# Weights' cycle of an eight-step software pipeline reordered, right products on two row tiles, and inverse roots by Newton steps

## The chip, the cores and the metric

The kernel runs on one core of a Trainium2 chip. The metric is the device time of one execution in microseconds (us), as the median over runs. TensorE is called PE, VectorE DVE, ScalarE ACT, GpSimd POOL and SyncE SP. SP computes nothing here: its queue issues nearly all DMAs.

## What is computed

A network of four layers on x of shape (4, 32, 32, 16), each `x = x + layer(groupnorm(x))`. Layers 0, 1 and 3 are position-dependent convolutions, layer 2 is an interval layer.

```python
# convolution layer (0, 1, 3): every position (i,j) has its own 3x3 kernel G[i,j] and its own weights W[i,j]
first   = einsum('ijyx,byxc->bijc', M, inputs)
shifted = conv(inputs, all 32*32*16 kernels of G)            # b, ij, yx, f
second  = einsum('ijyx,bijyxc->bijc', W, relu(inputs - shifted))
out     = first - second
# interval layer (2)
r = concat(running max, running min over intervals)          # b, 33, 33, 32
f = max_k sigmoid(f[b,i,k] @ Wf + r[b,k,j] @ Wr + b)         # two such steps
out = sigmoid(concat(f, r) @ W2 + b2)
# group norm
(g - mean) / sqrt(var + 1e-5)                                # 8 groups of two channels
```

## The kernel before

**Phases and steps.** Two groups of two batches and three convolution layers give six *phases* (`phases`, L90). A phase goes over eight blocks of 128 positions (`t`), a block over 16 channels `f` and 2 batches `b`: 32 *steps* a block, 256 a phase, 1536 in all. A step computes one tile `pc` of 128 positions x 1024 pixels: `first_part` multiplies it up in matmuls with WL and WU (L658 to L663) and has ACT scale it; `second_part`, run one step later, adds the matmuls with WD and W9 and has DVE form min(., 0) times the position's weights, with a sum over pixels (L680). Every matmul uses 64 rows; the two halves of the rows work as two row tiles side by side. Four `pc` tiles exist (two PSUM banks each), and the interval layer's small products take their tiles from the same ring.

**Units.** The kernels of four channels make a *unit*, used for eight steps. The kernel computes in a split fp32: each unit has a high and a low part of its weights. Units 0 and 1 are used plainly; from unit 2 on `prep_parts` (L220) builds a unit in a *cycle* of eight calls, one at the start of each step (L718). Unit u's cycle begins 15 steps ahead of its first use, and its call c (1 to 8) stands c steps after step 8(u - 2), so 16 - c steps ahead of that use. In the first block the cycle starts at step 3, and two steps take an extra call. The calls:

| call | before |
|---|---|
| 1 | DVE: mask the weights to their high bits (`high`, L203) |
| 2 | ACT: half of W9 (`halve`, L175) |
| 3 | ACT: WD (L236); POOL: WL (L237), W9 (L238) |
| 4 | ACT: WU (L240); POOL: WD (L241), four copies between quarters of the rows (L243, L245) |
| 5 | POOL: `prep` of the next unit (L214) |
| 7 | SP: two DMAs copy `parts[:, 0]` with its row halves swapped into `parts[:, 1]` (L251), the *swap*; then the raw load of unit u + 2 (L110) |

PE reads `parts[:, 1]` from the second pair of matmuls of the unit's first step. There are three buffers of `parts` and of W9, two of `raw`.

**Work behind.** All other work (norms, taps, interval layer, first terms) is a generator, `behind` (L733). At the end of a step it may be continued: `yield n` waits n steps, `yield IDLE` waits for a step whose call allows it (calls 1, 5, 6, 7, 8), `yield CALM` for one of the calls 6 to 8. So order on every engine and queue is program order, fixed by these yields; nothing is reordered. `before_conv` (L368) prepares the next phase: group norm, transposes to `xt` (L375), 8 DMAs to DRAM (`inner`, L381), 24 DMAs that read the nine shifted images back (`taps`, L392), and per batch a split and 12 DMAs that place the parts (`place`, L290). In the first phase `rest_of_start` (L869) does a split and a `place` for each batch of the first group.

**Norms.** `group_norm` (L312) takes sums on DVE, differences on POOL, then Sqrt on ACT (L358) and a reciprocal on DVE. A dummy Sqrt on `spare` (L353) and a dummy Sigmoid (L591) bring ACT's function table in ahead of use.

**Interval layer.** `right_side` (L555) multiplies the right factors in three matmuls of 11 values of k each (352, 231 and 110 columns), all on rows 0 to 63, each in its own PSUM tile and in its own step, and ACT copies each into `rt`.

Of the kernel before, what the change touches and what calls it, by code (L numbers as in the profile page):

```python
# [15 lines left out]
P = 128  # L16
# [28 lines left out]
def net_kernel(ctx: ExitStack, tc: tile.TileContext, x, xq, xi, convs, iv_w, iv_b, out):  # L45
# [162 lines left out]
    def prep(u, at=0, to=FU, eng=nc.gpsimd):  # L208
# [4 lines left out]
        for s in range(2 if u < PLAIN else 1):  # L213
# [4 lines left out]
            )  # L218

    def prep_parts():  # L220

        for u in range(PLAIN, n_chunks * NU):
            parts = wpool.tile([P, 2, 3, FU, P], F32R, tag="parts", bufs=AHEAD + 1, name=f"parts_{u}")
            W9 = wpool.tile([P, FU, P], F32R, tag="W9", bufs=AHEAD + 1, name=f"W9_{u}")
            units[u] = [parts[:, :, k] for k in range(3)] + [W9]
            src = raws.pop(u)
            w8 = src[:, 0].rearrange("p f k -> p (f k)")  # L230
            WU, WL, WD = (parts[:, 0, k].rearrange("p f k -> p (f k)") for k in range(3))
            high = upper(src[:, 0:1], 1, f"w{u}")[:, 0]
            yield (IDLE,)
            halve(W9, src[:, 1], low_w)
            yield ()
            nc.scalar.activation(WD, high, AF.Copy, scale=-EPS)  # L236
            nc.gpsimd.tensor_tensor(WL, w8, high, ALU.subtract)  # L237
            nc.gpsimd.tensor_tensor(W9, W9.bitcast(F32), src[:, 2], ALU.add)  # L238
            yield ()
            nc.scalar.copy(WU, high)  # L240
            nc.gpsimd.tensor_tensor(WD, WD.bitcast(F32), WL.bitcast(F32), ALU.add)  # L241
            for lo, hi in QUARTERS:
                nc.gpsimd.tensor_copy(WU[hi], WL[lo].bitcast(F32))  # L243
            for lo, hi in QUARTERS:
                nc.gpsimd.tensor_copy(WL[lo], high[hi])  # L245
            yield ()
            prep(u + 1)
            yield (IDLE,)
            yield (IDLE, CALM)
            for h in range(2):  # L250
                nc.sync.dma_start(  # L251
                    parts[64 * h : 64 * h + 64, 1].bitcast(F32),
                    parts[64 - 64 * h : 128 - 64 * h, 0].bitcast(F32),
                )
            load_raw(u + RAWS)
            yield (IDLE, CALM)
            yield (IDLE, CALM)

# [50 lines left out]
    def pair_view(ap):  # L309
        return ap.rearrange("p t (g s) -> p t g s", s=2)  # L310

    def group_norm(g, name, dst, gap):  # L312

# [104 lines left out]
    def first_terms(layer, mt):  # L418
# [27 lines left out]
    def constants():  # L446
# [6 lines left out]

        nc.gpsimd.tensor_scalar_mul(mask2[GC : 2 * GC], mask2[GC : 2 * GC], -1.0)
        yield 2
# [22 lines left out]
        for k, name in ((1, "r0"), (4, "r1")):  # L478
            t = const.tile([64, NQ * GB, C], F32, name=name)
            for q in range(NQ):  # L480
                blocks(t[:, q * GB : (q + 1) * GB, :], k, mask2, GB)
            iv[name] = t.rearrange("p k c -> p (k c)")
            yield 1
    def interval_layer(g):
# [37 lines left out]
        def running(dst, src):  # L522
# [17 lines left out]
            fill=0.0, base=0, channel_multiplier=0,  # L540
        )
        yield 5

# [11 lines left out]
        def right_side(name, wr):  # L555

            for k0 in range(0, T1, 11):
                j0 = k0 + 1
                ps = bank(f"ps_{name}{g}{k0}")
                n = T1 - j0  # L560
                nc.tensor.matmul(  # L561
                    ps[:, : 11 * n], lhsT=wr, rhs=r[:R, k0 : k0 + 11, j0:], start=True, stop=True
                )
                nc.scalar.copy(
                    rt[:, j0:, k0 : k0 + 11],
                    ps[:, : 11 * n].rearrange("p (k j) -> p j k", j=n),
                )
                yield 1

        def step(name, ftp, bias):  # L570
# [19 lines left out]
            yield IDLE  # L590
            nc.scalar.activation(spare, spare, AF.Sigmoid)  # L591
            yield 2
# [114 lines left out]
    def conv_layer(phase, behind):  # L707
# [4 lines left out]
        for t in range(NT):  # L712
# [267 lines left out]
```

## Time and profile before

| | |
|---|---|
| median of 3 runs | 2478.37 us (2478.1 to 2479.17) |
| the profiled execution | 2478.41 us |
| its span, first to last instruction | 2476.7 us |
| PE busy | 2458.2 us, 99% |
| DVE busy | 2087.3 us, 84% |
| ACT busy | 1878.4 us, 76% |
| POOL busy | 1579.7 us, 64% |
| ACT table loads | 5, 1283 ns each |
| swap DMAs (L251) | 380, 384 KB each, median 4.9 us from issue to landing |
| raw loads (L110) | 190, 768 KB each, 7.1 us |

Matmul ends are modelled, so PE's busy share is read together with the starts of the matmuls: a step begins every 1.566 us on PE in the steady part. In phase 3, step 224 begins on PE at 1600.3 us; times of other steps of that phase follow from it, since PE hardly waits there. A group's line gives line, engine, operation, output<-inputs, shapes, count, then busy time and mean, then the idle time before it and what ended it. A timeline line gives start and duration in us, engine, line, operation, output<-input and count; for "SPq" it is the time that SP took to issue the DMAs, waits between them included. A wait's line gives who waited for whom, then the total in us, how often, and the longest.

### The profile page before, as it was taken

The numbers are of one execution on the slowest core, as the hardware profiler recorded it, in microseconds if no ns is written. First come the engines' busy times: TensorE is split into PE (matmuls) and PEld (weight loads), VectorE is DVE, ScalarE is ACT, GpSimd is POOL, SyncE is SP. The second block draws the span as 40 slices with busy tenths as digits, with TensorE's granted clock in tenths as the row PEclk, the third lists the DMA queues.
The fourth block names the chain that finished last, engine by engine and source line by source line (L and its number), as shares of the span: only waits on it lengthen the run. The fifth ranks groups of instructions, "written<-read, shape, count | busy, mean of one in ns | idle before, by whom it ended". The sixth has DMA issues, their size and how long they took to land.

```text
span 2476.7 us, 58058 instructions
## 1 busy us (share of the span) xinstructions
PE 2458.2 (99%) x21906; PEld 2090.1 (84%) x21906; DVE 2087.3 (84%) x3617; ACT 1878.4 (76%) x2181; POOL 1579.7 (64%) x1750
## 2 busy tenths in 40 slices
PE   8999999999999999999999999999999999999999
PEld 5999888888888888888888988888998888888887
DVE  9888878888888888778898988899889888788887
ACT  4778767787777778777777777787777787677776
POOL 4766655666565657555567777586878676555552
PEclk9999999999999999999999999999999999999999
DMA  6446754466454467644454545574455467554442
GB/s 198 138 137 182 203 155 135 124 182 164 133 143 135 135 168 198 186 116 134 136 145 127 142 124 140 146 196 125 126 138 144 127 181 195 154 148 137 137 137 54
DMA packets 97673, 366.92 MB, mean 148 GB/s; under 512 B 26480, under 2 KB 31472, under 8 KB 97392
## 3 DMA queue, kind: packets, MB, share of 16 engines
q1 hardware_dynamic: 96832, 362.79, 53.0%
q8 instruction: 172, 2.82, 0.5%
q14 instruction: 109, 0.89, 0.1%
q10 hardware_dynamic: 432, 0.39, 0.1%
q0 software_dynamic: 128, 0.02, 0.0%
HBM read 199.78 MB, written 1.02 MB: 81 GB/s over the span
## 4 chain that ended last, share of the span: by engine, by line
PE 94%; DVE 2%; issue 1%; DMA 1%; ACT 0%; SPq 0%; POOL 0%; ACTq 0%; DVEq 0%; POOLq 0%
PE pc L627 93%; DVE junk L680 1%; PE pf L425 1%; DMA raw<-in_g 1%; ACT pc L663 0%; DMA first<-in_g 0%; SPq L298 0%; DVE raw L846 0%; SPq L300 0%; PE ps_l L548 0%; PE ps_r L561 0%; DMA parts<-parts 0%; DVE tables L508 0%; DVE raw L854 0%; DMA ib<-first 0%
## 5 line engine op out<-in xcount | busy, mean ns | idle before, releaser
L680 DVE SCALAR_TENSOR_TENSOR junk<-pc,WT 128x1024 f32<-128x1024 f32 x1536 | 1879.5, 1224 | 359.1 <-PE pc L627 308.3
L663 ACT ACTIVATE pc<-pc 128x1024 f32<-128x1024 f32 x1520 | 1532.0, 1008 | 561.0 <-PE pc L627 535.8
L627 PE MATMUL pc<-ib,parts 64*128 64x512 f32 x6080 | 958.5, 388 | 4.1 <-DVE junk L680 3.4
L627 PE MATMUL pc<-iyz,parts 64*128 64x512 f32 x6080 | 955.5, 387 | 2.2 <-ACT pc L663 2.0
L627 PE MATMUL pc<-ia,parts 64*128 64x496 f32 x6080 | 933.5, 379 | 0.0
L627 PEld LDWEIGHTS pc<-ia,parts 64*128 64x128 f32 x6080 | 595.5, 184 | 100.8
L627 PEld LDWEIGHTS pc<-ib,parts 64*128 64x128 f32 x6080 | 591.5, 184 | 105.0 <-DVE junk L680 9.9
L627 PEld LDWEIGHTS pc<-iyz,parts 64*128 64x128 f32 x6080 | 592.5, 184 | 88.4 <-ACT pc L663 6.4
L627 PE MATMUL pc<-im,W 64*128 64x496 f32 x3072 | 611.5, 384 | 0.0
L237 POOL TENSOR_TENSOR parts<-raw,upper_w 128x512 fp32r<-128x512 f32 x190 | 248.5, 1308 | 500.2 <-DVE upper_w L203 434.8
L627 PEld LDWEIGHTS pc<-im,W 64*128 64x128 f32 x3072 | 303.0, 184 | 54.5 <-issue 3.2
L243 POOL CAST parts<-parts 32x512 fp32r<-32x512 f32 x380 | 231.1, 608 | 50.1 <-ACT parts L240 31.8
L238 POOL TENSOR_TENSOR W<-W,raw 128x512 fp32r<-128x512 f32 x190 | 247.6, 1303 | 1.8 <-ACT W L175 1.8
L241 POOL TENSOR_TENSOR parts<-parts 128x512 fp32r<-128x512 f32 x190 | 246.8, 1299 | 2.0 <-ACT parts L236 1.9
L245 POOL CAST parts<-upper_w 32x512 fp32r<-32x512 f32 x380 | 231.6, 609 | 22.8
L214 POOL TENSOR_TENSOR raw<-raw,ident 128x512 f32<-128x512 f32 x190 | 199.9, 1052 | 52.2 <-DMA raw<-in_g 28.7
L175 ACT ACTIVATE W<-raw,low_w 128x512 fp32r<-128x512 f32 x190 | 136.2, 717 | 0.1
L680 DVE DVE_READ_ACCUMULATOR junk<-pc,WT 128x1 f32 x1536 | 127.5, 83 | 0.0
L236 ACT ACTIVATE parts<-upper_w 128x512 fp32r<-128x512 f32 x190 | 118.8, 625 | 6.6 <-DVE upper_w L203 6.4
L240 ACT CAST parts<-upper_w 128x512 fp32r<-128x512 f32 x190 | 116.5, 613 | 0.0
L695 POOL TENSOR_SCALAR acc<-acc 128x32 f32<-128x32 f32 x40 | 16.4, 409 | 141.7 <-DVE junk L680 139.7
L203 DVE TENSOR_SCALAR upper_w<-raw 128x512 int32<-128x512 int32 x190 | 86.1, 453 | 1.2 <-POOL raw L214 0.9
(139 smaller groups left out, 479.4 us busy)
## 6 DMA issues: line engine op xcount, KB each, us to landing
raw<-in_g SPq DMA_DIRECT2D x190, 768.0 KB, 7.1
parts<-parts SPq DMA_DIRECT2D x380, 384.0 KB, 4.9
WT<-in_w SPq DMA_DIRECT2D x48, 512.0 KB, 4.6
MT<-in_mt SPq DMA_DIRECT2D x24, 512.0 KB, 7.4
raw<-xs SPq DMA_DIRECT2D x120, 71.8 KB, 2.9
ib<-temp SPq DMA_DIRECT2D x40, 128.0 KB, 2.6
ia<-temp SPq DMA_DIRECT2D x80, 62.0 KB, 3.4
ib<-first SPq DMA_DIRECT2D x8, 128.0 KB, 2.4
```

Of the source, the lines that this page charges most:

```text
L175: nc.scalar.activation(dst, src, AF.Copy, scale=mask[:, 1:2])
L214: eng.tensor_tensor(raws[u][:, s, at:to], raws[u][:, s, at:to], pick[s][:, f0 + at : f0 + to].unsqueeze(2).to_broadcast([P, to - at, P]), ...
L236: nc.scalar.activation(WD, high, AF.Copy, scale=-EPS)
L237: nc.gpsimd.tensor_tensor(WL, w8, high, ALU.subtract)
L238: nc.gpsimd.tensor_tensor(W9, W9.bitcast(F32), src[:, 2], ALU.add)
L240: nc.scalar.copy(WU, high)
L241: nc.gpsimd.tensor_tensor(WD, WD.bitcast(F32), WL.bitcast(F32), ALU.add)
L243: nc.gpsimd.tensor_copy(WU[hi], WL[lo].bitcast(F32))
L245: nc.gpsimd.tensor_copy(WL[lo], high[hi])
L627: nc.tensor.matmul(ps[:, h, at : at + n], lhsT=w[r], rhs=v[r] if n == NH else v[r][:, :n], start=first and k == 0, stop=k == len(pairs) - ...
L663: nc.scalar.activation(ps, ps, AF.Copy, scale=1.0 + EPS)
L680: nc.vector.scalar_tensor_tensor(junk, ps.rearrange("p h n -> p (h n)"), 0.0, chunks[n], op0=ALU.min, op1=ALU.mult, accum_out=accs[phase][ ...
```

## The change

The weights' cycle has the same number of calls and of operations, in a new order:

| call | after |
|---|---|
| 1 | ACT: half of W9 |
| 2 | DVE: `high`, in a tile of its own; SP: the swap of the *previous* unit |
| 3 | ACT: WD; POOL: WL |
| 4 | ACT: WU; POOL: W9, `prep` of the next unit |
| 5 | POOL: WD, the four copies; SP: the raw load of unit u + 2 |

`IDLE` is now allowed at calls 2, 5, 6, 7, 8. The norm's inverse root is a shift and a subtraction on the bits (DVE), followed by four Newton steps of four small operations each on POOL; the dummy Sqrt, the Sqrt and the reciprocal go, and with them two of the yields. A single dummy Sigmoid in layer 0's `first_terms` takes the place of those in the interval steps. The right factors' weights are laid on all 128 rows, the table `r` is copied to rows 64 to 127 (`below`), and the three right matmuls are issued together, the first on the upper rows, the other two on the lower, into one pair of banks. `squares` lies in the buffer of `junk`.

```diff
+    def exchange(parts):
+        if parts is not None:
+            for h in range(2):
+                nc.sync.dma_start(
+                    parts[64 * h : 64 * h + 64, 1].bitcast(F32),
+                    parts[64 - 64 * h : 128 - 64 * h, 0].bitcast(F32),
+                )
...
+        swapped = None
         for u in range(PLAIN, n_chunks * NU):
...
-            high = upper(src[:, 0:1], 1, f"w{u}")[:, 0]
-            yield (IDLE,)
             halve(W9, src[:, 1], low_w)
             yield ()
+            high = work.tile([P, FU * P], F32, tag="high", bufs=2, name=f"high_{u}")
+            nc.vector.tensor_scalar(
+                high.bitcast(I32), w8.bitcast(I32), HIGH, None, op0=ALU.bitwise_and
+            )
+            exchange(swapped)
+            yield (IDLE,)
             nc.scalar.activation(WD, high, AF.Copy, scale=-EPS)
             nc.gpsimd.tensor_tensor(WL, w8, high, ALU.subtract)
-            nc.gpsimd.tensor_tensor(W9, W9.bitcast(F32), src[:, 2], ALU.add)
             yield ()
             nc.scalar.copy(WU, high)
+            nc.gpsimd.tensor_tensor(W9, W9.bitcast(F32), src[:, 2], ALU.add)
+            prep(u + 1)
+            yield ()
             nc.gpsimd.tensor_tensor(WD, WD.bitcast(F32), WL.bitcast(F32), ALU.add)
...
-            yield ()
-            prep(u + 1)
+            load_raw(u + RAWS)
+            swapped = parts
             yield (IDLE,)
-            yield (IDLE, CALM)
-            for h in range(2):
-                nc.sync.dma_start(
...
-            load_raw(u + RAWS)
-            yield (IDLE, CALM)
-            yield (IDLE, CALM)
+            for _ in range(3):
+                yield (IDLE, CALM)
+        yield (IDLE, CALM)
+        exchange(swapped)
...
+    def inverse_root(v, name):
...
+        nc.gpsimd.tensor_scalar(a, v, 1.0 / (2 * NP), 1e-5, op0=ALU.mult, op1=ALU.add)
+        nc.vector.tensor_scalar(
+            t.bitcast(I32), a.bitcast(I32), 1, None, op0=ALU.logical_shift_right
+        )
+        nc.vector.tensor_scalar(
+            y.bitcast(I32), t.bitcast(I32), -1.0, float(0x5F3759DF), op0=ALU.mult, op1=ALU.add
+        )
+        nc.gpsimd.tensor_scalar_mul(a, a, -0.5)
+        for pause in (1, 1, IDLE, 2):
+            yield pause
+            nc.gpsimd.tensor_tensor(t, a, y, ALU.mult)
+            nc.gpsimd.tensor_tensor(t, t, y, ALU.mult)
+            nc.gpsimd.tensor_scalar(t, t, 1.5, None, op0=ALU.add)
+            nc.gpsimd.tensor_tensor(y, y, t, ALU.mult)
+        return y
...
-        nc.scalar.activation(spare, spare, AF.Sqrt)
         v = yield from totals(f"v{name}")
-        yield 2
-        yield IDLE
-        rstd = work.tile([P, GC // 2], F32, tag="rstd", name=f"rstd_{name}")
-        nc.scalar.activation(rstd, v, AF.Sqrt, bias=eps, scale=1.0 / (2 * NP))
-        yield 2
-        nc.vector.reciprocal(rstd, rstd)
+        rstd = yield from inverse_root(v, name)
...
+        if layer == 0:
+            nc.scalar.activation(spare, spare, AF.Sigmoid)
...
+        below = tables[R:, : T1 * T1].rearrange("p (i j) -> p i j", j=T1)
+        nc.gpsimd.tensor_copy(below, r[:R])
+        tops = (r[:R], below)
         yield 5
...
-            for k0 in range(0, T1, 11):
+            ps = bank_pair(f"ps_{name}{g}")
+            blocks = []
+            for k0, h, at in ((0, 0, 0), (11, 1, 0), (22, 1, 11 * (T1 - 12))):
                 j0 = k0 + 1
-                ps = bank(f"ps_{name}{g}{k0}")
                 n = T1 - j0
+                blocks.append((k0, j0, n, ps[:, h, at : at + 11 * n]))
                 nc.tensor.matmul(
-                    ps[:, : 11 * n], lhsT=wr, rhs=r[:R, k0 : k0 + 11, j0:], start=True, stop=True
+                    blocks[-1][3], lhsT=wr[R * h : R * h + R], rhs=tops[h][:, k0 : k0 + 11, j0:],
+                    start=True, stop=True,
                 )
+            for k0, j0, n, sums in blocks:
                 nc.scalar.copy(
...
                 yield 1
...
             yield IDLE
-            nc.scalar.activation(spare, spare, AF.Sigmoid)
             yield 2
...
-                if n == 0 and at in (20, 24):
+                if n == 0 and at in (17, 20):
                     next(parts)
...
-    squares = const.tile([P, 256], F32, name="squares")
+    squares = work.tile([P, NP], F32, tag="junk", name="squares")[:, :256]
```

More of the change, by code (lines that the diff above doesn't have):

```diff
@@ L245, in prep_parts @@
                 nc.gpsimd.tensor_copy(WL[lo], high[hi])
-            yield ()
-            prep(u + 1)
+            load_raw(u + RAWS)
+            swapped = parts
             yield (IDLE,)
-            yield (IDLE, CALM)
-            for h in range(2):
[L251 to L254, printed above, removed]
-            load_raw(u + RAWS)
-            yield (IDLE, CALM)
-            yield (IDLE, CALM)
+            for _ in range(3):
+                yield (IDLE, CALM)
+        yield (IDLE, CALM)
+        exchange(swapped)
     def prep_plain(u, at=0, to=FU, eng=nc.gpsimd):
@@ L310, in pair_view @@
         return ap.rearrange("p t (g s) -> p t g s", s=2)
+    def inverse_root(v, name):
+        n = GC // 2
+        a, y, t = (
+            work.tile([P, n], F32, tag=tag, name=f"{tag}_{name}") for tag in ("root_a", "root_y", "root_t")
+        )
[5 more added lines that the diff above has]
+            y.bitcast(I32), t.bitcast(I32), -1.0, float(0x5F3759DF), op0=ALU.mult, op1=ALU.add
+        )
+        nc.gpsimd.tensor_scalar_mul(a, a, -0.5)
[6 more added lines that the diff above has]
+        return y
     def group_norm(g, name, dst, gap):
@@ L452, in constants @@
         )
-        nc.gpsimd.tensor_scalar_mul(mask2[GC : 2 * GC], mask2[GC : 2 * GC], -1.0)
+        for at in (GC, 3 * GC):
+            nc.gpsimd.tensor_scalar_mul(mask2[at : at + GC], mask2[at : at + GC], -1.0)
         yield 2
@@ L478, in constants @@
         for k, name in ((1, "r0"), (4, "r1")):
-            t = const.tile([64, NQ * GB, C], F32, name=name)
+            t = const.tile([P, NQ * GB, C], F32, name=name)
             for q in range(NQ):
@@ L555, in right_side @@
         def right_side(name, wr):
-            for k0 in range(0, T1, 11):
+            ps = bank_pair(f"ps_{name}{g}")
+            blocks = []
+            for k0, h, at in ((0, 0, 0), (11, 1, 0), (22, 1, 11 * (T1 - 12))):
                 j0 = k0 + 1
-                ps = bank(f"ps_{name}{g}{k0}")
                 n = T1 - j0
+                blocks.append((k0, j0, n, ps[:, h, at : at + 11 * n]))
                 nc.tensor.matmul(
-                    ps[:, : 11 * n], lhsT=wr, rhs=r[:R, k0 : k0 + 11, j0:], start=True, stop=True
+                    blocks[-1][3], lhsT=wr[R * h : R * h + R], rhs=tops[h][:, k0 : k0 + 11, j0:],
+                    start=True, stop=True,
                 )
+            for k0, j0, n, sums in blocks:
                 nc.scalar.copy(
-                    rt[:, j0:, k0 : k0 + 11],
-                    ps[:, : 11 * n].rearrange("p (k j) -> p j k", j=n),
+                    rt[:, j0:, k0 : k0 + 11], sums.rearrange("p (k j) -> p j k", j=n)
                 )
```

## The prediction

> **What bounds the kernel.** I read the page first (engines, then the chain), then the waits, then the timeline of the DMA queue of SP. The profiled execution took 2478.41 us for a span of 2476.7, the median of the runs is 2478.37: the sum below starts from 2478.4.
>
> ```profile
> span 2476.7 us, 58058 instructions
> PE 2458.2 (99%) x21906; PEld 2090.1 (84%) x21906; DVE 2087.3 (84%) x3617; ACT 1878.4 (76%) x2181; POOL 1579.7 (64%) x1750
> ...
> PE 94%; DVE 2%; issue 1%; DMA 1%; ACT 0%; SPq 0%; POOL 0%; ACTq 0%; DVEq 0%; POOLq 0%
> ```
>
> PE is the bound. A pair of matmuls (one on each row half) starts every 223 ns at 512 columns and every 216 ns at 496, so a step of 4 + 3 pairs takes 1.54 us at least and in fact 1.566. All gaps between matmuls beyond that pace add up to some 11 us after t = 50 us. So the change can win little; it can lose whatever it makes PE wait.
>
> What PE needs from SP is each unit's swapped copy, `parts[:, 1]`. The tile `parts` has this line for its DMAs:
>
> ```profile
> DMA to landing us min/median/max: 3.5/4.9/7.6
> ```
>
> Between the issue of the second swap DMA and PE's use of it lie 14.4 us (median over 190 units), but only 6.3 to 8.5 in ten units. These ten come where SP has other DMAs in its queue:
>
> ```profile
> SPq L251 <- POOL parts L245: 539.2, 164, 8.3
> ...
> SPq L381 <- DVE xt L375: 35.7, 5, 7.8
> ...
> SPq L392 <- DMA raw<-in_g: 20.9, 8, 3.0
> ```
>
> Usually SP stands at L251 and waits for POOL's copies: a later place in the program costs nothing then. But the third line says that tap loads (L392) wait for a `raw` load: a DMA stands until the one eight places before it has landed. The timeline of SP ahead of step 224 of phase 3:
>
> ```profile
> 1581.78 5.26 SPq L381 DMA_DIRECT2D xs<-xt  x8
> 1587.82 5.70 SPq L392 DMA_DIRECT2D raw<-xs  x12
> 1593.68 1.11 SPq L251 DMA_DIRECT2D parts<-parts  x2
> 1594.84 1.36 SPq L110 DMA_DIRECT2D raw<-in_g  x1
> 1596.24 9.90 SPq L392 DMA_DIRECT2D raw<-xs  x12
> 1606.29 1.10 SPq L251 DMA_DIRECT2D parts<-parts  x2
> ```
>
> Swaps are stuck between 12 tap DMAs and 12 more, in program order. PE enters step 224 at 1600.3, so the swap issued at 1593.68 just makes it. And at the start:
>
> ```profile
> 32.77 1.29 SPq L300 DMA_DIRECT2D ib<-first  x2
> 34.16 1.19 SPq L251 DMA_DIRECT2D parts<-parts  x2
> 35.39 1.21 SPq L110 DMA_DIRECT2D raw<-in_g  x1
> 36.69 3.33 SPq L298 DMA_DIRECT2D ia<-first  x4
> 40.08 1.29 SPq L300 DMA_DIRECT2D ib<-first  x2
> 41.42 5.84 SPq L298 DMA_DIRECT2D ia<-first  x4
> 47.31 1.29 SPq L300 DMA_DIRECT2D ib<-first  x2
> ```
>
> Unit 2's swap goes out between the placing of batch 0 and that of batch 1; PE starts on unit 2 at 43.33.
>
> **What the Trainium skill says.** "ScalarE: Activation LUTs" (What ACT_TABLE_LOAD costs): a change of table set is a load of about 1283 ns; the trace agrees (1283 ns, 5 loads). "TensorEngine Tiling (Array Packing)" (Key Properties): different tiles load weights and multiply in parallel; the trace agrees, both row halves start within 4 ns. "TensorE: Matmul & The Clock Gate" (Part 1): after an idle window of about 3.4 us the clock falls to half until about 3.4 us of work have passed; no gap of that length is in the body of this trace, so no row shows it.
>
> **The change, part by part.**
>
> *Roots by Newton.* Per norm it removes two Sqrt activations and a reciprocal and puts 18 operations of [128,16] on POOL and two on VectorE: 18 x 0.25 us (row L344, 253 ns) = 4.5 us, 36 us over 8 norms. POOL is 897 us idle, so I cost them at nothing; without that cover each norm would come up to 4.5 us late to its consumer, which stands 3 steps later. Four table loads go:
>
> ```profile
> 1420.18 1.28 ACT L591 ACT_TABLE_LOAD   x1
> ...
> 1421.58 1.89 ACT L663 ACTIVATE pc<-pc 128x1024 f32<-128x1024 f32 x2
> ```
>
> The load holds back ACT's scaling of `pc`, and PE's next `iyz` matmul is 0.55 us late and the one after 0.11. So at 1422.6, 1566.5, 1834.4 and 1978.2: 4 x 0.66 = **-2.6 us**. The one new load (Sigmoid, layer 0) lies under 7.0 us of first-term matmuls, when ACT has nothing to do: 0, at worst +0.7.
>
> *Right products on two row tiles.* Three insertions per call, four calls. From the first `ps_r` matmul to the `ps_l` matmuls PE takes 1.46 to 1.61 us more than its pace. Together, one half does 352 columns in two passes (0.60 us measured), the other 231 + 110 in 2 x (0.20 + 0.10) = 0.60: about 0.7 with a 0.1 us restart. 4 x 0.8 = **-3.2 us** (-1.5 to -4). The copy `below` (1089 elements; 1.3 us by row L243, 2.3 by L534) sits on POOL ahead of a wait of 5 steps: 0.
>
> *Masking (`high`) one call later.* ACT's `WD` comes one call after it instead of two, so VectorE's lag reaches ACT, then PE. I compared, unit by unit, the end of the product sum that now stands ahead of the masking with ACT's start of `WD`. Usually 0.52 us remain. In 24 of 190 units (scans, reduces, `halve_rest`) the lag exceeds what ACT's idle (0.08) and PE's slack (0.29) absorb, by 6.6 us in sum; 2.9 of it lies where PE stands already. I take **+2** (0 to +4.5). `halve`, `W9`, `prep` and `squares` move without anyone waiting: 0, covered by POOL's idle and by 7 steps between a raw load and its use (6 before).
>
> *The swap three calls later.* This is what decides. I counted the yields by hand to see behind which DMAs each swap now stands (positions, no times; for before they agree with the trace: `inner` emitted at steps 101, 37 and 210 of phases 0, 1 and 3 is on SP 2.1 steps later each time). A unit's swap was emitted 9 steps ahead of its first use, now 6.
>
> Start: `place` of batch 1 is emitted at step 11, unit 2's swap at step 12 (before: 9). It now stands behind 12 placing DMAs. Raw load 4 goes first, at 34.1; the placing starts at 35.4, 12 x 0.64 us plus up to 1.5 us for the raw landing: the swap's second half is issued at 45.0 to 46.3 and lands 4.5 us later, at 49.5 to 50.8. PE needs it at 43.6. That is 6 to 7 us, less 0.9 that PE waited at 50.5 for batch 1: **+5.6** (+4 to +7.5).
>
> Phases 3 and 4 (interval layers; `inner` now at step 204, taps at 206 to 211): the swap needed at step 216 is emitted at 210, behind 8 `inner` DMAs, raw load (205) and 16 tap DMAs. Before, it was emitted at 207, ahead of all of these. In steps: `inner` on SP 206.1 to 209.1, raw 209.1, the eighth tap DMA 5.3 later (raw landing, as measured) 214.4, nine more at 0.3 to 217.1, the second half 217.4, landed 220.4. PE needs it at 216.1: 4.3 steps = 6.7 us (5.4 to 8.7), twice: **+13.4**. Each phase's `place` of batch 0 then adds 0.5 step: +0.8 x 2 = **+1.6**.
>
> Phase 0: swap at 106 behind `inner`, raw and 12 taps lands at 112.8, needed 112.1: +1.0; that behind `place` (128) lands at 136.7, needed 136.1: +0.9. Phases 1, 2: swap at 50 lands at 56.6, needed 56.1: +0.8 each. Sum **+3.5** (0 to +8).
>
> *Clock.* Three of these waits exceed 3.4 us. By the page named above each may cost a window at half clock, an estimated 1.7 us: **+5** (0 to +9).
>
> Sum: -2.6 - 3.2 + 2 + 5.6 + 13.4 + 1.6 + 3.5 + 5 = +25.3, so 2503.7; I say **2503**.
>
> **Rivals.** (1) *The swaps arrive in time.* Then -2.6 - 3.2 + 2 = -3.8 remain, 2474.6, or 2472.6 if ACT absorbs the masking: at the edge of faster or just beyond. For it speaks the median slack of 14.4 us, which exceeds a landing by 9.5; against it, that slack is gone exactly where taps and placing stand in the queue. It decides at one place: the swap for step 216 must be issued before step 213.2. That needs 24 DMAs and a raw load in 7 steps, which took 11 or more in the trace. (2) *Only the start is late*, since the taps get through faster than in the trace: -3.8 + 5.6 + 1 = 2481, within 0.2%. (3) *ACT and the clock are worse*: every long wait ends cold and VectorE's lag reaches PE in all 24 units: +4.5 and +9 instead of +2 and +5, with the swaps at their upper ends: 2518 and more. (4) *POOL becomes the bound* through the root operations: 36 us spread over 8 norms against 897 idle; only if it delays the copies by over 5 us does PE see it; nothing speaks for it.
>
> **How the numbers follow.** A measurement of this kernel can tell about 0.2% (5 us) from no change: below 2473.4 is faster, above 2483.3 slower. Late swaps in phases 3 and 4: 0.77, which with its unknowns gives 2487 to 2518. Rival 3: 0.07, above 2516. Rival 2: 0.06. Rival 1: 0.10, mostly under 2473.4. So faster 0.08, same 0.08, slower 0.84. The range 2480 to 2518 leaves out rival 1 and the far end of rival 3.
>
> **What would show it.** Right: among PE's waits the DMA `parts<-parts`, about 6 us near 44 us and about 7 us in each interval phase at step 216 (about 1600 and 2010 us), and the swap on SP behind 16 taps. ACT table loads fall from 5 to 2 and the four gaps of 0.66 us vanish; `ps_r` matmuls come in one cluster. Matmuls at double duration right after the long waits show the clock. Wrong: no wait of PE on `parts<-parts` over 2 us after t = 60 us; or a swap that SP issues ahead of the taps; or a loss that sits in many waits on ACT or VectorE.

## The result, and the profile after

The changed kernel takes 2544.35 us (median; 2541.52 to 2548.45), the kernel before 2478.57 on the same chip: a ratio of 1.0267 (95% interval 1.0251 to 1.0283), or some 66 us more. The forecast was 2503 with a range of 2480 to 2518: right in sign, too small by 41 us. The profiled execution of the changed kernel took 2541.52 us.

In the changed kernel the matmuls stand at L661, the masking at L244, WD at L249, ACT's scaling of `pc` at L697, the swap at L223, `inner` at L407 and the taps at L418. From the page, span and engines:

```profile
span 2539.2 us, 58013 instructions
...
PE 2481.3 (98%) x21906; PEld 2107.9 (83%) x21906; DVE 2088.4 (82%) x3625; ACT 1872.6 (74%) x2159; POOL 1602.8 (63%) x1897
```

PE has the same 21906 matmuls as before, DVE and ACT are busy about as long, and POOL is busy 23 us more. What grows is PE's waiting. It stands before `ib` for the swap, as forecast, and before `iyz` for ACT, which was forecast at almost nothing. The waits of the same kernel (us in total, times, longest) give the chain behind the second: ACT waits for the masking, PE for ACT.

```profile
ACT parts L249 <- DVE high L244: 38.2, 40, 4.1
...
PE pc L661 <- DMA parts<-parts: 22.5, 17, 4.2
...
PE pc L661 <- ACT pc L697: 17.0, 24, 1.8
```

In the kernel before, PE never waits for `parts<-parts`, its waits for ACT's scaling add up to 2.0 us, and ACT's waits for the masking to this:

```profile
ACT parts L236 <- DVE upper_w L203: 6.4, 5, 2.8
```

**The swap** at step 216 of phase 3, where the forecast put it. SP's queue, then PE's timeline:

```profile
1605.93 3.79 SPq L407 DMA_DIRECT2D xs<-xt  x8
1610.13 0.35 SPq L110 DMA_DIRECT2D raw<-in_g  x1
1610.78 11.11 SPq L418 DMA_DIRECT2D raw<-xs  x16
1622.05 1.10 SPq L223 DMA_DIRECT2D parts<-parts  x2
```

```profile
1621.29 0.39 PE L661 MATMUL pc<-ib,parts 64*128 64x512 f32 x2
1625.83 0.79 PE L661 MATMUL pc<-ib,parts 64*128 64x512 f32 x1 [4.15 <-DMA parts<-parts]
1627.76 0.79 PE L661 MATMUL pc<-ib,parts 64*128 64x512 f32 x1 [1.14 <-DMA parts<-parts]
```

The swap goes out behind `inner`, a raw load and 16 taps. PE waits twice, once for each row half, since the two DMAs land one after the other, and comes back with matmuls of 0.79 us instead of 0.39. PE's granted clock falls to half during the first wait and stays there for 6.8 us (stretches of the same kernel; the number after the busy times is the granted clock):

```profile
core 0: us, PE busy (x) PEld busy (x) DVE busy (x) ACT busy (x) POOL busy (x), PEclk, DMA share, GB/s
1621.03:1624.45 3.42, 0.65 (x6) 0.19 (x4) 1.42 (x4) 0.80 (x1) 0.95 (x2) 1.00 0.71 173
1624.45:1627.86 3.41, 0.89 (x3) 0.39 (x3) 0.00 (x0) 0.00 (x0) 0.00 (x0) 0.50 0.94 221
1627.86:1631.28 3.42, 3.42 (x16) 2.73 (x18) 0.54 (x1) 1.55 (x2) 0.00 (x0) 0.50 0.88 180
```

**The masking** near 1380 us, on DVE, ACT and PE in turn:

```profile
1379.72 0.08 DVE L714 DVE_READ_ACCUMULATOR junk<-pc,WT 128x1 f32 x1
1379.72 1.28 DVE L622 TENSOR_REDUCE s_a<-tables 128x33 f32<-128x1089 f32 x1
1380.92 0.69 DVE L244 TENSOR_SCALAR high<-raw 128x512 int32<-128x512 int32 x1
```

```profile
1381.64 0.63 ACT L249 ACTIVATE parts<-high 128x512 fp32r<-128x512 f32 x1 [1.23 <-DVE high L244]
1382.18 1.01 ACT L697 ACTIVATE pc<-pc 128x1024 f32<-128x1024 f32 x1
```

```profile
1383.24 0.73 PE L661 MATMUL pc<-iyz,parts 64*128 64x512 f32 x4 [0.74 <-ACT pc L697]
```

A reduction that the interval layer emitted behind call 1 stands on DVE directly ahead of the masking of call 2. ACT's WD (call 3) waits 1.23 us for it, the scaling of `pc` stands behind WD in ACT's queue, and PE waits 0.74 us for that. Before the change one call more lay between masking and WD, and the reduction came after the masking.

**Where the time goes.** DVE makes one product sum per step, in all kernels in the same order. The lag of its end behind that of the kernel before (one profiled execution each) grows as follows, in us. Two columns show the swap and the masking moved alone in the kernel before, the last the changed kernel with both put back (the runs are described below):

| phase | after | swap alone (b1) | masking alone (b2) | both put back (a3) |
|---|---|---|---|---|
| 0 | 13.9 | 13.4 | 7.1 | 3.6 |
| 1 | 7.0 | 7.8 | 2.0 | 0.4 |
| 2 | 6.9 | 10.6 | 2.8 | 0.1 |
| 3 | 17.0 | 9.7 | 16.5 | 2.1 |
| 4 | 17.8 | 14.2 | 18.6 | 5.0 |
| 5 | 0.1 | 0.0 | 0.0 | 0.3 |

The swap costs in all five phases that prepare a next one; the masking mostly in phases 3 and 4, where the interval layer's long reductions and scans stand on DVE. Of the 17.0 us that PE waits for ACT in the changed kernel, 13.4 lie in these two phases.

### The profile page after: what moved, and what is told of

Read it like the earlier page. It is cut to its first block, busy times and chain, and to the rows that moved or that the text cites. A ratio compares the mean times of both kernels' runs of the same rounds, so it can differ in the third digit from the quotient of the medians.

```text
span 2539.2 us, 58013 instructions
## 1 busy us (share of the span) xinstructions
PE 2481.3 (98%) x21906; PEld 2107.9 (83%) x21906; DVE 2088.4 (82%) x3625; ACT 1872.6 (74%) x2159; POOL 1602.8 (63%) x1897
## 5 line engine op out<-in xcount | busy, mean ns | idle before, releaser
L697 ACT ACTIVATE pc<-pc 128x1024 f32<-128x1024 f32 x1520 | 1532.2, 1008 | 592.0 <-PE pc L661 573.8
L661 PE MATMUL pc<-ib,parts 64*128 64x512 f32 x6080 | 983.0, 389 | 27.8 <-DMA parts<-parts 22.5
L661 PE MATMUL pc<-iyz,parts 64*128 64x512 f32 x6080 | 976.9, 389 | 17.5 <-ACT pc L697 17.0
L661 PE MATMUL pc<-ia,parts 64*128 64x496 f32 x6080 | 953.4, 380 | 0.0
L661 PEld LDWEIGHTS pc<-ib,parts 64*128 64x128 f32 x6080 | 612.1, 185 | 131.1 <-DMA parts<-parts 31.4
L661 PEld LDWEIGHTS pc<-ia,parts 64*128 64x128 f32 x6080 | 613.0, 185 | 96.2
L661 PEld LDWEIGHTS pc<-iyz,parts 64*128 64x128 f32 x6080 | 598.2, 184 | 112.8 <-ACT pc L697 37.1
L250 POOL TENSOR_TENSOR parts<-raw,high 128x512 fp32r<-128x512 f32 x190 | 246.7, 1299 | 667.4 <-PE pc L661 526.8
L661 PE MATMUL pc<-im,W 64*128 64x496 f32 x3072 | 625.6, 385 | 0.0
L661 PEld LDWEIGHTS pc<-im,W 64*128 64x128 f32 x3072 | 317.2, 185 | 53.0 <-issue 3.3
L260 POOL CAST parts<-high 32x512 fp32r<-32x512 f32 x380 | 234.8, 618 | 22.8
L214 POOL TENSOR_TENSOR raw<-raw,ident 128x512 f32<-128x512 f32 x190 | 198.3, 1044 | 1.6 <-DMA raw<-in_g 1.6
L249 ACT ACTIVATE parts<-high 128x512 fp32r<-128x512 f32 x190 | 119.3, 628 | 44.2 <-DVE high L244 38.2
L252 ACT CAST parts<-high 128x512 fp32r<-128x512 f32 x190 | 116.0, 611 | 0.0
L244 DVE TENSOR_SCALAR high<-raw 128x512 int32<-128x512 int32 x190 | 87.7, 461 | 0.1
```

Of the source, the lines that this page charges most:

```text
L214: eng.tensor_tensor(raws[u][:, s, at:to], raws[u][:, s, at:to], pick[s][:, f0 + at : f0 + to].unsqueeze(2).to_broadcast([P, to - at, P]), ...
L661: nc.tensor.matmul(ps[:, h, at : at + n], lhsT=w[r], rhs=v[r] if n == NH else v[r][:, :n], start=first and k == 0, stop=k == len(pairs) - ...
L697: nc.scalar.activation(ps, ps, AF.Copy, scale=1.0 + EPS)
```

## The experiments

Theory: two waits on PE, one on a late swap (SP's queue), one on ACT behind a late masking (DVE's queue). Rivals: one of them alone; a loss from POOL's root operations; a swap that is late by its lead alone, whatever the queue. Ratios are to the kernel before on the same chip (2478 to 2480.5 us there).

| run | edit | us | ratio (95%) |
|---|---|---|---|
| a1_swap_back | after, swap back at call 7 | 2521.18 | 1.0172 (1.0157 to 1.0187) |
| a2_mask_back | after, masking back at call 1 | 2531.77 | 1.0219 (1.0202 to 1.0236) |
| a3_both_back | after, both back | 2492.23 | 1.0053 (1.0038 to 1.0068) |
| a4_old_cycle | before, with roots, right products and `squares` of after | 2484.94 | 1.0020 (1.0011 to 1.0029) |
| b1_swap_alone | before, swap late | 2529.81 | 1.0205 (1.0190 to 1.0220) |
| b2_mask_alone | before, masking at call 2 | 2518.35 | 1.0161 (1.0143 to 1.0180) |
| b3_roots_alone | before, Newton roots | 2486.49 | 1.0030 (1.0018 to 1.0041) |
| b4_right_alone | before, right products | 2476.38 | 0.9991 (0.9983 to 1.0000) |
| d1_wd_early | before, WD at call 2 | 2505.45 | 1.0102 (1.0088 to 1.0116) |
| g1_mask_moved_apart | b2 with an empty call ahead of WD | 2487.88 | 1.0037 (1.0024 to 1.0051) |
| c1_after_apart | a1 with an empty call ahead of WD | 2506.98 | 1.0114 (1.0100 to 1.0128) |
| f1_two_swaps_on_act | b1, two swaps on ACT's queue | 2513.68 | 1.0133 (1.0119 to 1.0147) |
| e0_short_roots | b3, 13 operations on POOL instead of 18 | 2481.49 | 1.0003 (0.9995 to 1.0011) |
| g3_roots_spread | e0, DVE's root operations a step apart | 2480.60 | 1.0008 (1.0000 to 1.0016) |
| e1_short_roots_right | e0 and right products | 2478.68 | 0.9996 (0.9988 to 1.0004) |

### Taking the parts out of the changed kernel

```diff
# a1: the swap back, in the changed kernel (cut)
-            exchange(swapped)
...
-            for _ in range(3):
-                yield (IDLE, CALM)
+            yield (IDLE, CALM)
+            exchange(parts)
+            yield (IDLE, CALM)
...
```

```diff
# a2: the masking back, in the changed kernel (cut)
-            halve(W9, src[:, 1], low_w)
-            yield ()
             high = ...
+            yield (IDLE,)
+            halve(W9, src[:, 1], low_w)
             exchange(swapped)
-            yield (IDLE,)
+            yield ()
```

> The changed kernel with only the swap put back to call 7 of its own unit. Theory (two causes that add up: the late swap, some 30 us with restarts and half clock, and the later masking, some 24 us): 2514 us (2508 to 2522), PE's waits on the DMA parts<-parts under 2 us, ACT's waits on high unchanged at about 38 us. Rival A (the swap is nearly all of it, ACT's waits only follow from it): 2485 us or less. Rival B (the root operations on GpSimd hold everything up): 2540 us.

> The changed kernel with only the masking put back to call 1, with halve at call 2; the swap stays late. Theory: 2520 us (2512 to 2527), ACT's waits on high from 38 us to under 8 us, PE's waits on parts<-parts unchanged at about 22 us. Rival A: 2540 us or more. Rival B: 2544 us.

> The changed kernel with both swap and masking at their places of before; the order on GpSimd (W9 and prep ahead of WD and the copies), the earlier raw load, the roots and the right products stay as changed. Theory: 2474 us (2471 to 2480), below before by the roots and the right products. Rival B: over 2520 us.

Measured 2521.18, 2531.77 and 2492.23. All three lie above what was expected. From both back, the late masking adds 0.0119 in the ratio (29 us) and the late swap then 0.0095 (24 us); in the other order the swap adds 41 and the masking 12. The two overlap. With the masking undone PE waits 29.3 us on swaps instead of 22.5, which fits a PE that doesn't stand for ACT and so reaches a late swap earlier. With the swap back at call 7, PE still waits 8.6 us on swaps, where under 2 were expected: in a1 SP issues one of them at 1613.76, behind 20 taps that took 13.53 us, so call 7 is not ahead of the taps in the changed kernel.

And 13 us remain with both undone, where a gain had been forecast. Run a4, in the next section, has the whole cycle of before, with the same roots and right products; it is 5 us slower than the kernel before. So the other 8 us of a3 (ratio 1.0053 against 1.0020, with intervals that don't meet) come from what else the new cycle has: above all POOL's new order, in which W9 and `prep` stand ahead of WD and the copies, then the earlier raw load and the own tile for `high`. These were not separated.

### Each part alone in the kernel before

> The changed kernel with the whole weights' cycle of before: only the roots by Newton steps, the right products on two row tiles and the place of squares remain. Theory: 2472.7 us (2470 to 2476), the four gaps of 0.66 us at table loads gone and the right products 0.8 us shorter each. Rival B: over 2490 us.

> The kernel before with one edit: each unit's two swap DMAs are issued at call 2 of the next unit instead of call 7 of its own; masking, roots, right products and the place of the raw load stay as before. Theory A (the swap's late waits are hidden by nothing else here, as between the kernels with the masking undone: 2531.8 against 2492.2): +39, about 2519 (2512 to 2526), with PE waiting on the DMA parts<-parts for some 30 us in about 19 waits. Theory B (the prediction's sum by itself, 24.1 us of waits and 5 of half clock): 2509 (2503 to 2512).

> The kernel before with one edit: the halving of the second weight stands at call 1 and the masking at call 2, one call ahead of ACT's copy of it; the swap, roots and right products stay as before. Theory A (VectorE's work emitted behind a step stands right ahead of the masking, so ACT's copy of it is late, then the scaling of pc, then PE): +29 as between the kernel with only the swap undone and the one with both undone, about 2509 (2502 to 2515), with ACT waiting on VectorE's masking for some 40 us in about 40 waits. Theory B (the prediction's term: the lag exceeds the slack in 24 units and costs 2 us): 2482.5 (2480 to 2485).

> The kernel before with the norms' roots by Newton steps and one Sigmoid table load in layer 0, all else as before. Theory A (the prediction: four table loads of 0.66 us go, POOL's operations are covered): 2478 (2476 to 2480). Theory B (the norm's changed pauses shift all later behind-work against the calls, or POOL's operations hold VectorE, which is what made the kernel with roots and right products 4.4 us slower instead of 5.8 faster): 2486 (2483 to 2489), with over 10 us of PE's gaps after waits on VectorE instead of 5.

> The kernel before with the right products on two row tiles and POOL's copy of the table for the lower tile, all else as before. Theory A (the prediction: -0.6 us per call in four calls, as the kernel with roots and right products showed between ps_r and ps_l): 2478 (2476 to 2480). Theory B (the slower part of the kernel with both comes from here, by POOL's copy or by the three results taken together): 2485 (2482 to 2489).

Measured 2484.94, 2529.81, 2518.35, 2486.49 and 2476.38. Swap and masking cost 51 and 40 us alone, more than either theory had expected. In b1's profiled execution PE waits 33.0 us on swaps, in 19 waits as expected; matmuls at half clock add 14.6 us. The right products bring about what they should. The roots cost 7.4 us, and a4's loss is theirs.

**What the roots cost.** The yields of the norm add up as before (2, IDLE and 2 before; 1, 1, IDLE and 2 now), and later work stays at its steps: the reductions of the interval layer begin within 0.1 step of where they began before. So it is the operations. POOL's timeline in the kernel before, then in b3, in the norm of phase 3:

```profile
1269.62 1.30 POOL L237 TENSOR_TENSOR parts<-raw,upper_w 128x512 fp32r<-128x512 f32 x1 [5.45 <-DVE upper_w L203]
...
1276.18 1.04 POOL L214 TENSOR_TENSOR raw<-raw,ident 128x512 f32<-128x512 f32 x1
```

```profile
1272.49 0.20 POOL L318 TENSOR_SCALAR root_a_i<-whole_vi 128x16 f32<-128x16 f32 x1 [8.05 <-DVE whole_vi L359]
...
1273.21 1.30 POOL L237 TENSOR_TENSOR parts<-raw,upper_w 128x512 fp32r<-128x512 f32 x1
...
1281.85 0.22 POOL L331 TENSOR_TENSOR root_y_i<-root_y_i,root_t_i 128x16 f32<-128x16 f32 x1
1282.03 1.04 POOL L214 TENSOR_TENSOR raw<-raw,ident 128x512 f32<-128x512 f32 x1
```

DVE in b3, then its waits for `prep` in the kernel before and in b3:

```profile
1283.10 0.43 DVE L203 TENSOR_SCALAR upper_w<-raw 128x512 int32<-128x512 int32 x1 [2.02 <-POOL raw L214]
1283.45 1.21 DVE L697 SCALAR_TENSOR_TENSOR junk<-pc,WT 128x1024 f32<-128x1024 f32 x1
```

```profile
DVE upper_w L203 <- POOL raw L214: 0.9, 3, 0.3
```

```profile
DVE upper_w L203 <- POOL raw L214: 9.7, 8, 2.0
```

POOL's first root operation stands in program order ahead of WL of the next unit and waits for DVE's variance. This WL begins at 1273.21 instead of 1269.62: 3.6 us late. Two Newton steps of four operations, 1.2 us each, come on top before `prep` (L214), which is then 5.9 us late. In the kernel before `prep` ended 3.3 us ahead of the masking that needs it; here DVE's masking stands 2.02 us for it, the product sum behind it is late, and PE waits for a free slot of `pc`. PE's waits for DVE's product sums add up to 10.1 us in b3 and 3.4 before.

### The masking: place or distance

d1 leaves the masking at call 1 and moves only WD next to it, with the halving one call later. g1 and c1 move the masking and put an empty call behind it; the copies then come a call later too.

```diff
# d1, in the kernel before (cut)
     high = upper(src[:, 0:1], 1, f"w{u}")[:, 0]
     yield (IDLE,)
+    nc.scalar.activation(WD, high, AF.Copy, ...)
+    yield ()
     halve(W9, src[:, 1], low_w)
-    yield ()
-    nc.scalar.activation(WD, high, AF.Copy, ...)
```

```diff
# g1, in the kernel before (cut)
+    halve(W9, src[:, 1], low_w)
+    yield ()
     high = upper(src[:, 0:1], 1, f"w{u}")[:, 0]
     yield (IDLE,)
-    halve(W9, src[:, 1], low_w)
     yield ()
     nc.scalar.activation(WD, high, AF.Copy, ...)
...
-    yield ()
+    yield (IDLE,)
     prep(u + 1)
-    yield (IDLE,)
```

> The kernel before with one exchange of two ACT operations: WD (the scaled copy of the masked weight) at call 2 and the halving at call 3, instead of halving at 2 and WD at 3. The masking keeps its place at call 1; only the distance from it to WD shrinks from two calls to one. Theory A (the distance is the cause: VectorE's lag reaches ACT's in-order queue, then pc, then PE): slower like the kernel with the masking moved, 2512 (2500 to 2525), with ACT waiting on the masking in 30 or more places. Theory B (the masking's new place among the behind-work is the cause, not the distance): 2480 (2477 to 2484), with few waits of ACT on the masking.

> The kernel before with the halving at call 1 and the masking at call 2, as in the kernel with the masking alone moved (2518.4), but with an empty call after it: WD at call 4, the copies at 5, prep at 6, swap and raw load at 7 as before. The behind-work keeps its places. Theory A (the distance of masking and WD is all): ACT's waits on the masking fall from 42 places to under 12 as before; the swap's copies come one call later, which may cost some us: 2485 (2479 to 2491). Theory B (the masking's place among the behind-work costs the 13 us that lie between 2518 and the 2505 of the kernel with the distance alone): 2493 or more.

> The changed kernel with the swap at call 7 of its own unit (2521.2) and an empty call between masking (call 2) and WD (call 4), the copies then at call 6. Theory A (the distance is all): the level of the kernel with masking and swap both undone, 2492, and up to 8 more for the later copies ahead of the swap: 2495 (2489 to 2503). Theory B (place as well): 2506 or more.

ACT's waits on the masking, one line each from the waits of b2, d1, g1 and c1:

```profile
ACT parts L236 <- DVE upper_w L203: 42.3, 42, 4.1
```

```profile
ACT parts L234 <- DVE upper_w L203: 37.2, 37, 2.8
```

```profile
ACT parts L237 <- DVE upper_w L203: 8.9, 11, 3.2
```

```profile
ACT parts L248 <- DVE high L243: 3.9, 3, 3.2
```

One call between masking and WD: about 40 waits, whether the masking was moved (b2) or not (d1). Two calls: 11 and 3, though it was moved. So the distance is what makes ACT wait, in both directions. Its price is 25 us by d1. The other 14 us of b2 are read from the traces and were not tested. Its waits are longer singly (up to 4.1 us against 2.8); the granted clock falls to half six times in its body, which adds some 10 us, and never in d1; and PE waits 3.9 us on late swaps. The profiled execution of b2 took 2525 us, 7 above the median, so these parts are its upper end. In g1 9 us remain. c1's 2507 misses the expected 2495 and lies at its theory B, place as well: there the copies come a call later still than in a1, PE waits 10.9 us on swaps, and the clock falls five times. So for the changed kernel the distance is shown to end ACT's waits, but the empty call brings only 14 of the 29 us.

### The swap: the queue or the lead

```diff
# f1, in b1: the swaps of two units go out on ACT's queue, at the same step
-    exchange(swapped)
+    exchange(swapped, nc.scalar if u in (125, 157) else nc.sync)
```

> The kernel with the swap alone moved (2529.8), and the swaps of two units only, those needed at step 224 of phases 3 and 4, issued by ACT's DMA queue instead of SP's, at the same step. Theory A (they are late because SP has 8 inner and 24 tap DMAs ahead of them): PE's waits at about 1637 and 2059 (5.5 and 1.6 us each) go and with them the half clock that follows, about 2508 (2503 to 2516). Theory B (a lead of six steps is too short for POOL's copies and the landing, whatever the queue): 2527 to 2533.

Measured 2513.68: 16 us less than b1 (18 by the ratios) for two moved swaps of 190. SP's queue in b1 ahead of step 224 of phase 3, then DMA issues of ACT's queue in f1:

```profile
1625.21 8.24 SPq L400 DMA_DIRECT2D raw<-xs  x12
1633.62 1.11 SPq L223 DMA_DIRECT2D parts<-parts  x2
```

```profile
1614.64 0.50 ACTq L223 DMA_DIRECT2D parts<-parts  x1
1615.44 0.49 ACTq L223 DMA_DIRECT2D parts<-parts  x1
```

PE in b1 at this step:

```profile
1637.41 0.79 PE L635 MATMUL pc<-ib,parts 64*128 64x512 f32 x1 [5.32 <-DMA parts<-parts]
1639.25 0.79 PE L635 MATMUL pc<-ib,parts 64*128 64x512 f32 x1 [1.05 <-DMA parts<-parts]
```

In f1 PE does not stand at this step, and later swaps of phases 3 and 4, still on SP, cost it 0.4 to 1.6 us each. At these two places, then, six steps of lead are enough for copies and landing when nothing is queued ahead: it is the queue.

In phases 0 to 2 the queue is not all of it. After the start b1 has six late swaps there, and five of them land 6.9 to 8.7 us after the issue of their second DMA, where the median is 5.0. For the swap issued at 565.94 this is (in all of b1: 3.6/5.0/11.9):

```profile
DMA to landing us min/median/max: 7.0/7.5/8.0
```

Why these land late was not tested.

Elsewhere, in phase 1 of b1:

```profile
517.41 0.39 PE L635 MATMUL pc<-ib,parts 64*128 64x512 f32 x2
518.15 0.50 PE L635 MATMUL pc<-ib,parts 64*128 64x512 f32 x1 [0.36 <-DMA parts<-parts]
520.07 0.50 PE L635 MATMUL pc<-ib,parts 64*128 64x512 f32 x1 [1.41 <-DMA parts<-parts]
```

These two waits, 1.8 us in all, are followed by 3.4 us at half clock, which cost some 1.4 us more; the lag of this unit is 3.3 us. What the clock goes by is taken up below.

### Roots that cost less

e0 moves the first operation to DVE, gives POOL its first two steps later and makes three Newton steps; g3 also spreads DVE's three operations over three steps; e1 is e0 with the right products.

```diff
# e0, in b3
-    nc.gpsimd.tensor_scalar(a, v, 1.0 / (2 * NP), 1e-5, op0=ALU.mult, op1=ALU.add)
+    nc.vector.tensor_scalar(a, v, 1.0 / (2 * NP), 1e-5, op0=ALU.mult, op1=ALU.add)
...
+    yield 2
     nc.gpsimd.tensor_scalar_mul(a, a, -0.5)
-    for pause in (1, 1, IDLE, 2):
-        yield pause
+    for pause in (IDLE, 2, None):
...
# g3, in e0: "yield 1" ahead of each of DVE's next two operations, and no "yield 2"
```

> The kernel before with the roots by Newton steps, but the first operation moved from POOL to VectorE, POOL's next one two steps later with the first Newton step, and three Newton steps instead of four: 13 operations on POOL instead of 18. Theory A (in the kernel with roots alone POOL stood 8.0 us at root_a, ahead of the next unit's work, and its Newton steps delayed prep, for which VectorE's masking waited; both go): the four table loads' gain is seen, 2476.4 (2474 to 2479), DVE's waits on raw L214 under 2 us. Theory B (any root operations on POOL hold up the chain): 2483 to 2487.

> The kernel with short roots (2481.5), VectorE's three root operations one step apart instead of in one step. Theory A (three operations in one step, each held by POOL's running operation, make the product sums of that step late): the four table loads' gain is seen, 2477.5 (2475 to 2479.5), PE's gaps after waits on VectorE near 6 us instead of 11. Theory B (the cost is not in their standing together): 2480 to 2483.

> The kernel with short roots, and the right products on two row tiles: the best version that the runs so far point to, with before's cycle, masking and swap. Theory A (the two gains of 2.6 us add up): 2473.8 (2471 to 2477), faster than both kernels. Theory B (the roots still cost): 2479 to 2485.

Measured 2481.49, 2480.60 and 2478.68. Most of b3's 7.4 us (0.0030) is gone in e0 (0.0003), and DVE's waits on L214 fall to 0.6 us. That fits POOL's order as the larger part, though e0 changes three things at once. The gain of the table loads doesn't show in the time: PE's waits for ACT do fall, from 2.0 us to 0.6, but those for DVE's product sums are still 9.2 us against 3.4. One reason to look at is DVE's first root operation. DVE and POOL of e0:

```profile
1270.87 1.31 DVE L318 TENSOR_SCALAR root_a_i<-whole_vi 128x16 f32<-128x16 f32 x1
1272.21 0.17 DVE L319 TENSOR_SCALAR root_t_i<-root_a_i 128x16 int32<-128x16 int32 x1
```

```profile
1270.84 1.30 POOL L241 TENSOR_TENSOR parts<-parts 128x512 fp32r<-128x512 f32 x1
```

16 elements a partition take 1.31 us on DVE, as long as POOL's operation that began 0.03 us before. The Trainium skill, "SBUF — State Buffer" (Who interferes with whom), says that `tensor_scalar` on DVE may use a pair of ports that it shares with GpSimd, and that whoever issues first holds the pair for the whole instruction; these times agree. g3, with the same 1.30 us but the three operations apart, is no faster: PE's waits for DVE's product sums fall from 9.2 to 6.3 us, which the time doesn't show. What the 3 to 5 us between these times and the expected ones are made of stays open. No version beats the kernel before by more than the measurement can tell; the right products alone come nearest.

## Why the prediction was wrong

Along a4, a3, a1 and the changed kernel the 66 us split as follows:

| part | forecast, us | measured, us |
|---|---|---|
| roots and right products (a4) | -5.8 | +5 |
| the rest of the new cycle, POOL's order above all (a3 beyond a4) | 0 | +8 |
| masking (a1 beyond a3) | +2 | +29 |
| swap with its clock (changed kernel beyond a1) | +29 | +24 |

The mechanism of the swap was right. The steps that failed are the masking's "+2", which was mis-sized and makes up most of the 41 us, and two terms of POOL that were put at nothing. In the other order of the runs, with the masking undone first, the masking counts 12 us and the swap 41.

**Right products: right.** -3.2 (-1.5 to -4) were forecast; alone they bring 0.0009 in the ratio, 2.2 us, at the edge of what can be told from nothing. From the first `ps_r` to `ps_l` PE now takes 0.93 to 1.04 us beyond its pace instead of 1.46 to 1.61; the estimate of 0.7 was a little low.

**Roots: wrong in sign.** The step that failed is "POOL is 897 us idle, so I cost them at nothing". The table loads did fall from 5 to 2, and PE's waits for ACT from 2.0 us to 0.4 in b3. But idle time over the whole span covers nothing at the place: POOL's chain WL, W9, WD, copies, `prep` feeds the next masking, with 3.3 us of slack in the norm of phase 3, and an operation that waits for DVE at the head of that chain moves it all. Rival 4, with its bound of 5 us of delay to the copies, had named the engine and dismissed it; b3 shows 3.6 + 2.3 us of delay to `prep`.

**POOL's order: put at nothing, cost 8 us.** "`halve`, `W9`, `prep` and `squares` move without anyone waiting: 0, covered by POOL's idle" failed in the same way. In a3 `prep` stands earlier and DVE's waits on it are gone, but the copies come one call later. Its trace has PE waiting 2.6 us for POOL's copies at the start and 4.3 us on late swaps (1.5 in a4), and DVE waiting 2.6 us for each of two `xn` and two `xi`. Which of these make up the 8 us is read from the trace and wasn't tested.

**Masking: the term that was mis-sized.** "24 of 190 units" was near in number: PE waits for ACT 24 times, whether or not in the same units. The 6.6 us of excess, and the +2 taken from them, were not: these waits are 17.0 us, with what follows 12 to 29 us in the changed kernel and 25 to 40 in the kernel before. The comparison took the product sum's end as the moment from which the masking can run. In the new order the behind-work of call 1, such as the reduction of 1.28 us near 1380, can stand between the two; before, it came after the masking. The trace of the kernel before could have told it: the right list to move the masking into was DVE's queue as it will stand, not as it stood.

**Swap: right in place, too small alone.** In the changed kernel it costs 24 us where 24.1 + 5 were forecast, and the single places fit: the lag grows by 6.5 us at the start (5.6 forecast and part of the clock), 7.6 and 7.5 at step 216 of phases 3 and 4 (6.7 each and clock). But 51 us alone, and 41 with the masking undone, show that this agreement is partly the masking's doing. Mis-sized were phases 0 to 2, "+3.5": by b1 they cost 13.4 less the 6.3 of the start, 7.8 and 10.6. Each has late swaps at two places, behind the taps and behind `place`, mostly with two waits, one for each row half, and in b1 five of these six swaps also landed late.

**Clock: the size in its range, the rule not.** The Trainium skill, "TensorE: Matmul & The Clock Gate" (Part 1), has the clock fall after an idle window of about 3.4 us, from which I counted three waits at 1.7 us each. The changed kernel has three falls in its body, each with 6.83 us at half clock; less the 4.7 us in which PE stood anyway, that is some 8 us at most, an estimate from the granted clock and PE's busy time. But no wait of 3.4 us is needed. At step 216 the clock fell 2.8 us into the first wait, and in b1 after the two waits of 1.8 us in all. Other waits of b1 brought no fall, such as one of 2.98 us that ended at 204.55. Its stretches show the difference (first two lines: the wait of 2.98 us; last two: the waits of 1.8 us and what came after):

```profile
199.89:203.31 3.42, 1.67 (x15) 1.06 (x11) 2.21 (x4) 1.03 (x2) 0.00 (x0) 1.00 0.94 192
203.31:206.72 3.41, 2.17 (x20) 1.85 (x22) 0.45 (x1) 1.01 (x1) 0.00 (x0) 1.00 0.48 115
517.33:520.75 3.42, 1.65 (x13) 0.84 (x11) 1.24 (x3) 0.62 (x1) 0.00 (x0) 1.00 0.73 147
520.75:524.16 3.41, 3.41 (x20) 2.74 (x18) 1.57 (x3) 1.04 (x2) 0.00 (x0) 0.50 0.65 205
```

In every trace here the falls lie whole multiples of 3.41 us apart, and half clock within the kernel's body lasts 3.41, 6.83 or 10.24 us. The stretches above are cut on this grid. Over all 17 traces, without the first 60 and the last 25 us, no stretch at full clock with less than 1.5 us of PE idle is followed by a fall, each of the 17 stretches with more than 1.9 us is, and of the 27 between these, 14 are. So what counts in these runs is PE's idle time within one stretch of the grid, not the length of a wait. A wait of 2.98 us that is split over two stretches (1.74 + 1.24 us) costs only itself, and 1.77 us within one costs half clock. So every late swap, not three, could cost some half clock: b1 has nine falls in its body.

**Rival 3** (ACT and clock worse) is the way it went, at a chance of 0.07. It was worked out from the same mis-sized numbers, so its 2518 was a lower end and not a middle.

**The sum** failed by its form, too: terms were added as if each acted alone. They don't add: 51 and 40 alone, 53 together.

## What to carry to other kernels

Before an operation is moved, write down its engine's queue as it will stand, with the small work of other stages in it, and count how far the consumer in another in-order queue follows: here one step of distance was worth 25 us, and an empty call gave most of it back in the kernel before, half of it in the changed one. Idle share of an engine covers nothing by itself; ask whether a waiting instruction stands ahead of a chain that feeds the bound. A transfer's lead is what is left after all that its queue holds in front of it.

## What was unexpected in the hardware

In these traces the clock goes down by PE's idle time within one stretch of a grid of 3.41 us, not by the length of a wait: 1.77 us in two waits within one stretch brought 3.41 us at half clock, 2.98 us in one wait over two stretches brought none. DVE's first root operation, a `tensor_scalar` on 128x16 elements, took 0.31 us at the least in e0 and 1.31 beside POOL's 1.30 us operation. Of the two DMAs of a swap, issued 0.5 us apart, the second lands 1.8 us after the first (medians of 190 in the changed kernel), so a late swap stops PE twice.
